# A deformable attention whose two images' and three rows' transfers are merged into single loads and stores

## The chip, the cores and the metric

The kernel runs on one core of one Trainium2 chip. The metric is device time in microseconds (us) of one execution, and the times of a kernel are given as the median of several. A core has the engines PE (TensorE, with PEld for its weight loads), DVE (VectorE), ACT (ScalarE), POOL (GpSimd) and SP (SyncE), and 16 DMA engines, which carry all transfers, whether SP, ACT or POOL issued them.

## The reference

The program is a small network over x of shape (2, 64, 64, 256): a deformable attention, a graph-routed mixture of 4 experts over 1,048,576 edges, a windowed attention, and a mixture of 8 experts. The change touches the first of the four alone:

```python
qkv = x @ qkv_w + qkv_b
qkv = _dwconv_nhwc(qkv, dw_w, dw_b)                     # depthwise 3x3, B, H, W, C = 2, 64, 64, 256
mask = einsum(pconv(q, mask_pconv_w), mask_w) + mask_b  # 9 per pixel
for g in range(8):                                      # groups of 32 channels, 9 taps each
    off = einsum(pconv(q, off_pconv_w[g]), off_w[g]) + off_b[g] + base[g]   # base: 3x3 taps, spread 2g+1
    k_g = flow_warp(k_map[group g], off) * mask         # bilinear samples of the map at the taps
    v_g = flow_warp(v_map[group g], off) * mask
attn = softmax((q / sqrt(32)) . k, over the 9 taps)
out = (attn . v) @ proj_w + proj_b
```

## The kernel before

`layernorm` (L235 to L242) and the matrix product of qkv go row by row to DRAM (`static_maps`, from L262). A second part of `static_maps` reads them back padded, makes the depthwise convolutions, and writes the maps of the attention to DRAM: queries `qd` by channel, column, row and image (L368), keys `kd` by channel and image with 16 repeated columns on each side (L434 and L436), values `vd` by group, image and row (L387), and the 153 offset and mask numbers of each pixel `offd` (L453). ACT writes each into its tile in transposed order (L366, L429, L452). In the same stretch DVE and PE sort the edges of the later mixture.

`static_attention` (from L456) then computes the attention without gathers. As an offset moves a tap by less than one pixel, the bilinear sample of a key, multiplied by the query, is a weighted sum of dot products at 3 x 3 shifts around the tap. So for each group three lanes of steps run one after another:

- `group_dots` (from L529): `queries` loads a half of the columns into `qt` (two column quarters and two images in four 32-partition blocks, one DMA each, L544), and DVE zeroes the image that a block isn't (L547). `keys` loads `kt` in the same blocks (L554, four DMAs). PE multiplies column by column (L564), ACT, at the very start also DVE, copies the result to a stage tile (L571), and ACT issues its store to `dots` in DRAM (L580).
- `group_weights` (from L590): `offsets` loads the offsets (12 DMAs, L632), `pick` and `read` load the dot products of three rows for each of the three tap rows into `lk` (L660), DVE multiplies them with the tent functions and adds (L694 to L708), takes the softmax, and forms the weights of each pixel on its 25 or 81 neighbours; POOL writes them to a matrix `wd` in DRAM (L773) and clears old ones (L788).
- `group_values` (from L842): `value_map` loads the values through `raw` (L859), DVE copies the images apart into `vt` (L861), POOL loads the matrices of `wd` into two `mat` tiles (L868), PE multiplies (L890), ACT copies the sum to `o` (L899), which has the same slot as `raw`, and issues its store to `od` (L903).

The loop `for n in range(-2, G)` takes the groups in the order 1 to 7, then 0, and runs the values of one group, the weights of the next and the dot products of the one after it in the same stage. Their steps are sorted by a fraction given by hand, and that is the order of the instructions on each engine. SP issues the loads of all three lanes in this order, so a load that waits for its buffer holds back all behind it. There are three `kt` buffers, two `qt`, two `lk`, one for offsets and one for `raw` and `o`.

`pick` has a rule for its pieces. A piece ends where the shifted row leaves the image, and one of more than 16 rows is cut to a multiple of 16:

```python
end = min(H, H - dy) if inside else (-dy if dy < 0 and y < -dy else H)
m = end - y
if m > 16:
    m -= m % 16
```

After the last group `project_out` loads `od` (L931) and multiplies by `proj_w`. A second path, `gathered` and `sample_attention`, runs only if an offset is larger than one pixel, which no input here has.

Of the kernel before, what the change touches and what calls it, by code (L numbers as in the profile page):

```python
# [23 lines left out]
F32 = mybir.dt.float32  # L24
# [97 lines left out]

def _shape_constants():
# [9 lines left out]
    grid = np.concatenate([grid.reshape(P, NOFF), np.zeros((P, K), np.float32)], 1)  # L133
# [31 lines left out]
    fold = np.concatenate([fold, own], 1)  # L165
# [15 lines left out]
class Net:  # L181
# [80 lines left out]
    def static_maps(self, maps, sort):  # L262
# [10 lines left out]
        with ExitStack() as ctx:  # L273
# [73 lines left out]
            with tc.tile_pool(name="mpad", bufs=2) as pads, tc.tile_pool(name="mq", bufs=1) as qp, \  # L347
# [12 lines left out]
                for b in range(B):  # L360
                    for j in range(CC):
                        for y in range(0, H, YC):
                            cv = kp.tile([P, YC, W], F32, name="cv")
                            self.dwconv(cv, padded("pad", j, b, y, YC), j, 0, YC)
                            to = q1[:, :, y : y + YC, b] if j else q0[:, 1 : W + 1, 1 + y : 1 + y + YC, b]
                            nc.scalar.copy(to.rearrange("p x y -> p y x"), cv)  # L366
# [43 lines left out]
                for j in range(CC):  # L410
# [5 lines left out]
                    for b in range(B):  # L416
                        km = kp.tile([P, W, H], F32, name="km", bufs=1)
                        for y in range(0, H, 8):
# [3 lines left out]
                            for tap in range(9):  # L422
# [7 lines left out]
                                km[:, :, y : y + 8].rearrange("p x y -> p y x"), ps, AF.Identity,  # L430
                                bias=bias,
                            )
                        to = kd[j * P : (j + 1) * P, b]
                        nc.sync.dma_start(to[:, BORDER : BORDER + W, :], km)  # L434
                        for at, src in ((0, 0), (BORDER + W, W - 1)):
                            nc.sync.dma_start(  # L436
                                to[:, at : at + BORDER, :], km[:, src : src + 1, :].to_broadcast([P, BORDER, H])
                            )
                XO = 8
                for x8 in range(0, W, XO):  # L440
                    off = op.tile([P, NOM, XO], F32, name="off")
                    for x in range(x8, x8 + XO, 2):
# [9 lines left out]
                        nc.scalar.copy(off[:, :, x - x8 : x - x8 + 2].rearrange("p n x -> p x n"), ps)  # L452
# [3 lines left out]
    def static_attention(self, maps, od, far):  # L456
# [7 lines left out]
        with ExitStack() as ctx:  # L464
# [12 lines left out]
            edge = one.tile([P, len(FOLDS) + B], F32, name="edge")  # L477
# [9 lines left out]
            def masks():  # L487

                masks = offd[:, NOFF:, :].rearrange("(y b) (kx ky) x -> b y ky kx x", b=B, kx=3)
                for b in range(B):  # L490
                    for ky in range(3):
                        nc.sync.dma_start(mask[H * b : H * b + H, 3 * ky : 3 * ky + 3, :], masks[b, :, ky])
                v = mask.rearrange("p (ky kx) x -> p ky kx x", ky=3)
                ob = self.row("offb")[:, NOFF:].rearrange("p (kx ky) -> p ky kx", kx=3)
                nc.vector.tensor_tensor(v, v, ob.unsqueeze(3).to_broadcast([P, 3, 3, W]), ALU.add)
                for t in mats + [none, pools["vt"]]:
                    nc.gpsimd.memset(t, 0.0)

            for n in range(-2, G):
                lanes = []  # L500
                if n >= 0:
                    g = ORDER[n]
                    lanes.append((lambda f: 0.12 + 0.88 * f, self.group_values(g, vd, wd[n % 2], mats, none, sums, od, pools)))
# [7 lines left out]
                if n + 2 < G:  # L511
                    g = ORDER[n + 2]
                    lanes.append((lambda f: 0.95 * f, self.group_dots(g, qd, kd, edge[:, len(FOLDS) :], dots, pools, n < 0)))
# [12 lines left out]
    def group_dots(self, g, qd, kd, own, dots, pools, alone):  # L526
# [12 lines left out]
        def queries(h):  # L539
            box["q", h] = qt = pools["one"].tile([P, XQ, H, B], F32, name="qt", bufs=2)  # L540
            for j in range(2):
                for b in range(B):
                    x, p0 = XH * h + XQ * j, 64 * j + 32 * b
                    nc.sync.dma_start(qt[p0 : p0 + HC], qd[g * HC : (g + 1) * HC, x : x + XQ])  # L544
# [4 lines left out]
        def keys(h, dx):  # L549
            box[h, dx] = kt = two.tile([P, XQ + 2, H], F32, name="kt", bufs=3)  # L550
            for j in range(2):
                for b in range(B):
                    x, p0 = BORDER + XH * h + XQ * j + dx, 64 * j + 32 * b
                    nc.sync.dma_start(kt[p0 : p0 + HC], kd[g * HC : (g + 1) * HC, b, x : x + XQ + 2])  # L554
# [45 lines left out]
    def group_weights(self, g, offd, mask, low, edge, s, wd, none, pools):  # L600
# [24 lines left out]
        def offsets():  # L625
            src = offd[:, g * 2 * K : (g + 1) * 2 * K, :].rearrange(
                "(y b) (kx ky two) x -> b y two ky kx x", b=B, kx=3, ky=3
            )
            for b in range(B):
                for i in range(2):  # L630
                    for ky in range(3):
                        nc.sync.dma_start(t5[H * b : H * b + H, 1, i, 3 * ky : 3 * ky + 3, :], src[b, :, i, ky])  # L632

        def bias(i):
            v = t5[:, 1, i].rearrange("p (ky kx) x -> p ky kx x", ky=3)
            ob = self.row("offb")[:, g * 2 * K : (g + 1) * 2 * K].rearrange("p (kx ky two) -> p two ky kx", kx=3, ky=3)
            nc.vector.tensor_tensor(v, v, ob[:, i].unsqueeze(3).to_broadcast([P, 3, 3, W]), ALU.add)
# [7 lines left out]
        def pick(to, dy, first, blocks, n):  # L645

            for b in range(B):
                y = 0
                while y < H:
                    ky = min(max(y + dy, 0), H - 1)  # L650
                    inside = 0 <= y + dy < H
                    end = min(H, H - dy) if inside else (-dy if dy < 0 and y < -dy else H)
                    m = end - y
                    if m > 16:
                        m -= m % 16
                    src = bass.AP(
                        s.tensor, s.offset + y * stride + b * (stride // B) + first * block + ky * line,
                        [[stride + (line if inside else 0), m], [block, blocks], [1, n * XH]],
                    )
                    nc.sync.dma_start(to[H * b + y : H * b + y + m], src)  # L660
                    y += m

        def read(ky):
            box[ky] = lk = two.tile([P, 3, 6, 3, XH], F32, name="lk")
            for sy in range(3):
                pick(lk[:, sy].rearrange("p k s x -> p k (s x)"), (ky - 1) * r + sy - 1, 0, 6, 3)

        def read_near():
            flat = two.tile([P, 27 * W], F32, name="ln", tag="lk")
            box["all"] = lk = flat[:, 0 : 25 * W].rearrange("p (y h s x) -> p y h s x", y=5, h=2, s=5)  # L670
            box["l"] = two.tile([P, 3, 6, 3, XH], F32, name="l4", tag="lk")
# [7 lines left out]
        def in_x(ky):  # L679
            tx = t5[:, :, 0, 3 * ky : 3 * ky + 3, :]  # L680
            if near:
                lk, box[ky] = box["all"], box["l"]
                for sy in range(3):
                    out = box[ky][:, sy].rearrange("p (k h) s x -> p h k s x", h=2)
# [8 lines left out]
            for sy in range(3):  # L693
                nc.vector.tensor_tensor(box[ky][:, sy], box[ky][:, sy], tx, ALU.mult)  # L694

        def sum_x(ky, i):
            l = box[ky].rearrange("p y k s x -> p (y k) s x")
            nc.vector.tensor_tensor(l[:, :, 0], l[:, :, 0], l[:, :, i], ALU.add)

        def in_y(ky):  # L700
            l = box[ky][:, :, :, 0, :]
            ty = t5[:, :, 1, 3 * ky : 3 * ky + 3, :].rearrange("p s k (h x) -> p s (k h) x", h=2)
            nc.vector.tensor_tensor(l, l, ty, ALU.mult)

        def sum_y(ky):
            l = box[ky][:, :, :, 0, :]
            nc.vector.tensor_tensor(l[:, 0], l[:, 0], l[:, 1], ALU.add)
            nc.vector.tensor_tensor(halves(lg[:, 3 * ky : 3 * ky + 3, :]), l[:, 0], l[:, 2], ALU.add)  # L708
# [90 lines left out]
        step(lambda: bias(0))  # L799
        step(lambda: bias(1))  # L800
# [41 lines left out]
    def group_values(self, g, vd, wd, mats, none, sums, od, pools):  # L842
# [11 lines left out]
        def value_map():  # L854
            wb, x0 = W + 2 * (r + 1), BORDER - (r + 1)
            for x in range(0, wb, 32):
                n = min(32, wb - x)
                raw = pools["one"].tile([P, 32, HC], F32, name="raw", tag="raw")
                nc.sync.dma_start(raw[:, 0:n, :], vd[g].rearrange("b y x c -> (b y) x c")[:, x0 + x : x0 + x + n, :])  # L859
                for b in range(B):  # L860
                    nc.vector.tensor_copy(vt[H * b : H * b + H, x : x + n, b, :], raw[H * b : H * b + H, 0:n, :])  # L861

        def load(n):
            h, kx, _ = runs[n]
            for b in range(B):
                for y in range(0, H, BAND):
                    lo, hi = band(g, y)
                    nc.gpsimd.dma_start(mats[n % 2][H * b + y : H * b + y + BAND, lo:hi], wd[y : y + BAND, b, 2 * kx + h, lo:hi])  # L868
# [28 lines left out]
        def end(h):  # L897
            o = pools["one"].tile([P, XQ, H], F32, name="o", tag="raw")
            nc.scalar.copy(o, sums[h])  # L899
            for q in range(2):  # L900
                for b in range(B):
                    x, p0 = XH * h + XQ * q, 64 * q + 32 * b
                    nc.scalar.dma_start(od[g * HC : (g + 1) * HC, b, x : x + XQ], o[p0 : p0 + HC])  # L903
# [1586 lines left out]
```

## Time and profile before

| | us |
|---|---|
| median of 3 runs | 6144.45 (6142.08 to 6149.82) |
| profiled execution, its time | 6110.76 |
| profiled execution, its span | 6109.0 |
| first attention, from the first keys load to the copy of the last group's result | 1172 to 2872 |

| engine | busy us (share of the span) |
|---|---|
| PE | 4115.2 (67%) |
| DVE | 2467.9 (40%) |
| ACT | 1154.1 (19%) |
| POOL | 1470.7 (24%) |

The profile is of one execution. A busy share is the time in which an engine had an instruction in work. A row of the groups table names a line, an engine, an operation, output <- input, their count, the busy time and mean duration, and the idle time before them with what ended it. A waits line names who waited for whom, the total, the number of waits and the longest. The DMA engines' packets are recorded with their queue (q1: SP, q10: ACT, q0: POOL), size and duration. The sum of a change is made against the profiled execution's own span; the median of the runs is 35 us above it.

### The profile page before, as it was taken

The page shows a single profiled execution, that of the slowest core. Times are in us where ns is not written, and L with a number is a line of the kernel's source. Part 1 is how long each engine was busy: PE and PEld are TensorE (multiplying, and loading weights), DVE is VectorE, ACT ScalarE, POOL GpSimd, SP SyncE. Part 2 cuts the span into 40 slices and gives each one's busy share as a digit, 9 for nine tenths or more (in the row PEclk, how much of TensorE's full clock was granted, in tenths as well). Part 3 has the DMA queues.
Part 4 walks back from the last instruction along what each step waited for, and adds up shares of the span by engine and source line. Part 5 has one row for each costly group of instructions (what it writes and reads, how often), then busy time and mean ns, then how long its engine had stood idle before and what let it go on. Part 6 is the DMA issues. An engine that isn't in the chain of part 4 may idle for free. (4 is left out here: it accounts for less than half of the span.)

```text
span 6109.0 us, 63383 instructions
## 1 busy us (share of the span) xinstructions
PE 4115.2 (67%) x22123; PEld 2876.5 (47%) x22123; DVE 2467.9 (40%) x5464; ACT 1154.1 (19%) x2302; POOL 1470.7 (24%) x1792
## 2 busy tenths in 40 slices
PE   7877688758265566354625680499947877769982
PEld 4655245745243444233412340388824444458872
DVE  6788985043121202220423473011155555532223
ACT  2110121122122222000100000122213343322210
POOL 1000001123342232443155414300062111110025
PEclk8776799868577777677867795699967888879986
DMA  6333367968678897787320001577621000058875
GB/s 179 97 102 113 99 171 148 66 152 179 126 159 175 176 188 155 120 142 126 84 13 4 4 2 64 173 225 223 194 86 40 22 21 22 21 184 263 263 235 159
DMA packets 775144, 759.72 MB, mean 124 GB/s; under 512 B 443959, under 2 KB 658935, under 8 KB 759317
## 3 DMA queue, kind: packets, MB, share of 16 engines
q1 hardware_dynamic: 576992, 412.37, 26.8%
q0 software_dynamic: 87008, 200.21, 16.9%
q10 hardware_dynamic: 110804, 142.87, 8.1%
q8 instruction: 182, 2.98, 0.2%
q14 instruction: 158, 1.29, 0.1%
HBM read 461.72 MB, written 296.60 MB: 124 GB/s over the span
## 5 line engine op out<-in xcount | busy, mean ns | idle before, releaser
L564 PE MATMUL dot<-kt,qt 64*128 64x192 f32 x2944 | 408.4, 411 | 479.1 <-ACT stage L571 320.8
L890 PE MATMUL acc<-mat,vt 128*64 128x192 f32 (+2 forms) x3680 | 491.7, 439 | 255.9 <-DMA mat<-wd 182.0
L564 PEld LDWEIGHTS dot<-kt,qt 64*128 64x128 f32 x2944 | 355.5, 235 | 535.7 <-ACT stage L571 340.5
L1658 PE MATMUL ps_h<-xgT,w1t 128*128 128x256 f32 x2240 | 545.0, 391 | 41.8 <-DVE xgT L1653 17.6
L1391 PE MATMUL ps<-oh,ol 128*128 128x512 f32 (+1 forms) x864 | 363.2, 584 | 240.8 <-issue 150.5
L1666 PE MATMUL ps_y<-w2t,hT 128*128 128x256 f32 x2240 | 513.9, 383 | 7.5 <-issue 4.4
L890 PEld LDWEIGHTS acc<-mat,vt 128*64 128x64 f32 x3680 | 310.3, 163 | 441.1 <-issue 318.1
L1658 PEld LDWEIGHTS ps_h<-xgT,w1t 128*128 128x128 f32 x2240 | 417.6, 193 | 122.8 <-DVE xgT L1653 26.2
L1666 PEld LDWEIGHTS ps_y<-w2t,hT 128*128 128x128 f32 x2240 | 430.0, 192 | 69.1 <-issue 5.2
L1661 ACT ACTIVATE hT<-ps_h,b1t 128x256 f32<-128x256 f32 x560 | 258.6, 473 | 846.4 <-PE ps_h L1658 756.7
L571 ACT COPY stage<-dot 128x384 f32<-128x384 f32 x640 | 269.5, 495 | 745.6 <-PE dot L564 295.2
L1669 DVE TENSOR_TENSOR y<-ps_y,b2t 128x256 f32<-128x256 f32 x280 | 118.8, 424 | 648.2 <-PE ps_y L1666 493.7
L1391 PEld LDWEIGHTS ps<-oh,ol 128*128 128x128 f32 x864 | 179.6, 212 | 424.0 <-issue 319.9
L868 POOL DMA_DIRECT2D mat<-wd x368 | 179.8, 494 | 590.5 <-PE acc L890 390.5
L424 PE MATMUL ps_k<-padk,diag 128*128 128x512 f32 x576 | 266.1, 621 | 76.4 <-issue 50.2
L260 DVE SCALAR_TENSOR_TENSOR cv<-pad,colt,cv 128x2048 f32<-128x2048 f32 x128 | 293.8, 2347 | 1.3
L2286 POOL DMA_INDIRECT xs<-tn,sloti x128 | 124.2, 971 | 638.9 <-DVE slot L2284 592.7
L1753 POOL DMA_INDIRECT back<-ys,back_row x128 | 123.3, 964 | 621.9 <-DVE run L2271 548.6
L1275 PE MATMUL psc<-oh,ol 128*128 128x64 bf16 x1792 | 235.0, 305 | 55.6 <-DVE oh L1273 55.6
L1275 PEld LDWEIGHTS <-ol 128*128 128x128 bf16 x1792 | 224.9, 148 | 94.0 <-issue 54.9
L333 PE MATMUL ps_q<-xT,wq 128*128 128x512 f32 x384 | 217.7, 708 | 44.5 <-ACT stage L337 33.2
L1651 PE MATMUL ps_x<-ident,xg 128*128 128x128 f32 x560 | 85.0, 275 | 225.4 <-DMA xg<-xs 225.4
(401 smaller groups left out, 6112.7 us busy)
## 6 DMA issues: line engine op xcount, KB each, us to landing
w1t<-in_W SPq DMA_DIRECT2D x140, 512.0 KB
w2t<-in_W SPq DMA_DIRECT2D x140, 512.0 KB
xg<-xs SPq DMA_DIRECT2D x140, 256.0 KB
ys<-y ACTq DMA_DIRECT2D x140, 256.0 KB
kt<-kd SPq DMA_DIRECT2D x184, 144.0 KB
pr<-stage SPq DMA_DIRECT2D x16, 1584.0 KB
mat<-wd POOLq DMA_DIRECT2D x112, 192.0 KB
mat<-wd POOLq DMA_DIRECT2D x64, 288.0 KB
```

The costliest lines, as they stand in the source:

```text
L260: nc.vector.scalar_tensor_tensor(out, src, w, out, ALU.mult, ALU.add)
L333: nc.tensor.matmul(ps.rearrange("p a b -> p (a b)"), lhsT=wq[:, k, c * P : (c + 1) * P], rhs=xT[:, k, :], start=(k == 0), stop=(k == CC - 1),)
L424: nc.tensor.matmul(ps.rearrange("p a b -> p (a b)"), lhsT=diag[:, tap, :], rhs=pad[:, at : at + 8, tap % 3 : tap % 3 + W], start=(tap == 0 ...
L564: nc.tensor.matmul(ps[jj][:, i, :], lhsT=qt[at, i0 + i].rearrange("p y b -> p (y b)"), rhs=kt[at, i0 + i : i0 + i + 3, :].rearrange("p s y ...
L571: (nc.vector.tensor_copy if alone and jj else nc.scalar.copy)(box["d"][:, :, :, x : x + 2], ps[jj].rearrange("p i (s y) -> p y s i", s=3),)
L868: nc.gpsimd.dma_start(mats[n % 2][H * b + y : H * b + y + BAND, lo:hi], wd[y : y + BAND, b, 2 * kx + h, lo:hi])
L890: nc.tensor.matmul(sums[h][64 * q : 64 * q + 64, j - 2 + a : j - 2 + c, :].rearrange("p x y -> p (x y)"), lhsT=vt[:, r + 1 + XH * h + XQ * ...
L1275: nc.tensor.matmul(psc, lhsT=ol[:, :, j], rhs=oh[:, :, j], start=(c1 == 0), stop=(c1 == NW - 1),)
L1391: nc.tensor.matmul(psf[:, c : c + m], lhsT=ol, rhs=ohf[:, c : c + m], start=(start and j == 0), stop=(stop and j == n - 1),)
L1658: nc.tensor.matmul(ps, lhsT=w1t[:, k, f * P : (f + 1) * P], rhs=xT[:, k, :], start=(k == 0), stop=(k == CC - 1),)
L1661: nc.scalar.activation(hT[:, f, :], ps, AF.Gelu, bias=b1t[:, f : f + 1])
L1666: nc.tensor.matmul(ps, lhsT=hT[:, f, i * P : (i + 1) * P], rhs=w2t[:, f, :], start=(f == 0), stop=(f == NF - 1),)
```

## The change

Storage orders change so that transfers can be joined:

- *Keys*: `kd` becomes `[G, B, HC, WB, H]`, so that a group's two images follow each other, and one DMA loads all 128 partitions of `kt`. The stores of `kd` become one for each of four groups.
- *Queries*: one DMA for each column quarter, whose source repeats the 32 channels for both images with a step of 0.
- *Picks*: `lk` is ordered `[6, 3, 3, XH]`, and one piece takes three neighbouring rows at once (9 x 32 numbers instead of 3 x 32) where none of them leaves the image; rows at the border are loaded singly. The cut to multiples of 16 rows is dropped.
- *Offsets, mask*: the rows of the offset weights and biases are sorted on the host (`_offset_order`), so that a group's 18 numbers are in the order of the tile and one DMA for each image loads them.
- *Values, matrices*: partitions are in the order (row, image) instead of (image, row). One DMA loads a band of both images of a matrix, and `value_map` separates the images by multiplying all 128 partitions with a column of ones and zeros (`odd`), so `vt` need not be zeroed once.
- *Results*: `od` becomes `[G, B, HC, W, H]`, and one DMA stores a half.
- The ACT copies of `static_maps` write in the order of the tile and read transposed.

The core of the diff:

```diff
@@ static_maps
-                            nc.scalar.copy(to.rearrange("p x y -> p y x"), cv)
+                            nc.scalar.copy(to, cv.rearrange("p y x -> p x y"))
...
-                        to = kd[j * P : (j + 1) * P, b]
-                        nc.sync.dma_start(to[:, BORDER : BORDER + W, :], km)
...
+                        for g in range(4):
+                            to, part = kd[4 * j + g, b], km[g * HC : (g + 1) * HC]
+                            nc.sync.dma_start(to[:, BORDER : BORDER + W, :], part)
...
@@ group_dots
         def queries(h):
...
             for j in range(2):
-                for b in range(B):
-                    x, p0 = XH * h + XQ * j, 64 * j + 32 * b
-                    nc.sync.dma_start(qt[p0 : p0 + HC], qd[g * HC : (g + 1) * HC, x : x + XQ])
+                src = qd[g * HC :, XH * h + XQ * j :]
+                nc.sync.dma_start(
+                    qt[64 * j : 64 * j + 64].rearrange("p x y b -> p (x y b)"),
+                    bass.AP(src.tensor, src.offset, [[0, B], [W * H * B, HC], [1, XQ * H * B]]),
+                )
...
         def keys(h, dx):
             box[h, dx] = kt = two.tile([P, XQ + 2, H], F32, name="kt", bufs=3)
-            for j in range(2):
-                for b in range(B):
-                    x, p0 = BORDER + XH * h + XQ * j + dx, 64 * j + 32 * b
-                    nc.sync.dma_start(kt[p0 : p0 + HC], kd[g * HC : (g + 1) * HC, b, x : x + XQ + 2])
+            src = kd[g, :, :, BORDER + XH * h + dx :]
+            nc.sync.dma_start(
+                kt.rearrange("p x y -> p (x y)"),
+                bass.AP(src.tensor, src.offset, [[XQ * H, 2], [WB * H, B * HC], [1, (XQ + 2) * H]]),
+            )
@@ group_weights
+            src = offd[:, g * 2 * K : (g + 1) * 2 * K, :].rearrange("(y b) n x -> b y (n x)", b=B)
             for b in range(B):
-                for i in range(2):
-                    for ky in range(3):
-                        nc.sync.dma_start(t5[H * b : H * b + H, 1, i, 3 * ky : 3 * ky + 3, :], src[b, :, i, ky])
+                nc.sync.dma_start(t5[H * b : H * b + H, 1].rearrange("p i k x -> p (i k x)"), src[b])
...
-        def pick(to, dy, first, blocks, n):
+        def pick(to, dy, first, blocks, n, y0=0, y1=H):
             for b in range(B):
-                y = 0
-                while y < H:
+                y = y0
+                while y < y1:
                     ky = min(max(y + dy, 0), H - 1)
-                    inside = 0 <= y + dy < H
-                    end = min(H, H - dy) if inside else (-dy if dy < 0 and y < -dy else H)
-                    m = end - y
-                    if m > 16:
-                        m -= m % 16
+                    inside = 0 < y + dy < H - 1
+                    end = min(y1, H - 1 - dy) if inside else (min(y1, 1 - dy) if y + dy <= 0 else y1)
                     src = bass.AP(
                         s.tensor, s.offset + y * stride + b * (stride // B) + first * block + ky * line,
-                        [[stride + (line if inside else 0), m], [block, blocks], [1, n * XH]],
+                        [[stride + (line if inside else 0), end - y], [block, blocks], [1, n * XH]],
                     )
-                    nc.sync.dma_start(to[H * b + y : H * b + y + m], src)
-                    y += m
+                    nc.sync.dma_start(to[H * b + y : H * b + end], src)
+                    y = end
 
         def read(ky):
-            box[ky] = lk = two.tile([P, 3, 6, 3, XH], F32, name="lk")
+            box[ky] = lk = two.tile([P, 6, 3, 3, XH], F32, name="lk")
+            dy = (ky - 1) * r
+            y0, y1 = max(0, 1 - dy), min(H, H - 1 - dy)
+            pick(lk.rearrange("p k y s x -> p k (y s x)"), dy - 1, 0, 6, 9, y0, y1)
             for sy in range(3):
-                pick(lk[:, sy].rearrange("p k s x -> p k (s x)"), (ky - 1) * r + sy - 1, 0, 6, 3)
+                for lo, hi in ((0, y0), (y1, H)):
+                    pick(lk[:, :, sy].rearrange("p k s x -> p k (s x)"), dy + sy - 1, 0, 6, 3, lo, hi)
@@ group_values
                 for b in range(B):
-                    nc.vector.tensor_copy(vt[H * b : H * b + H, x : x + n, b, :], raw[H * b : H * b + H, 0:n, :])
+                    nc.vector.tensor_scalar(vt[:, x : x + n, b, :], raw[:, 0:n, :], odd[:, b : b + 1], None, ALU.mult)
...
-            for b in range(B):
-                for y in range(0, H, BAND):
-                    lo, hi = band(g, y)
-                    nc.gpsimd.dma_start(mats[n % 2][H * b + y : H * b + y + BAND, lo:hi], wd[y : y + BAND, b, 2 * kx + h, lo:hi])
+            for y in range(0, H, BAND):
+                lo, hi = band(g, y)
+                nc.gpsimd.dma_start(
+                    mats[n % 2][B * y : B * (y + BAND), lo:hi].rearrange("p h s x -> p (h s x)"),
+                    wd[y : y + BAND, :, 2 * kx + h, lo:hi].rearrange("y b h s x -> (y b) (h s x)"),
+                )
...
-            for q in range(2):
-                for b in range(B):
-                    x, p0 = XH * h + XQ * q, 64 * q + 32 * b
-                    nc.scalar.dma_start(od[g * HC : (g + 1) * HC, b, x : x + XQ], o[p0 : p0 + HC])
+            to = od[g, :, :, XH * h :]
+            nc.scalar.dma_start(
+                bass.AP(to.tensor, to.offset, [[XQ * H, 2], [W * H, B * HC], [1, XQ * H]]), o.rearrange("p x y -> p (x y)")
+            )
```

## Prediction

> **What bounds the kernel now.** I first read the windows view, cut at the ends of the eight groups' results in the first attention (the copies of L899), to see which stretch the change can touch and whether an engine is full in it.
>
> ```profile
> 0.00:1172.00 1172.00, 934.75 (x4467) 642.67 (x4468) 825.08 (x1548) 200.90 (x275) 92.97 (x142) 0.82 0.54 121
> 1320.00:1532.00 212.00, 142.41 (x1022) 101.65 (x1024) 69.30 (x91) 50.16 (x114) 84.90 (x110) 0.76 0.79 157
> 1532.00:1845.00 313.00, 147.07 (x1059) 108.36 (x1055) 67.66 (x83) 64.81 (x148) 115.65 (x143) 0.70 0.73 141
> 2486.00:2663.00 177.00, 68.09 (x488) 46.66 (x486) 63.30 (x94) 5.37 (x6) 75.08 (x120) 0.69 0.83 133
> 2663.00:2787.00 124.00, 69.36 (x489) 45.51 (x489) 19.21 (x17) 2.15 (x3) 63.97 (x109) 0.75 0.73 112
> ```
>
> The columns are the window, its length, then busy us of PE, PEld, DVE, ACT and POOL, the clock, the DMA engines' mean busy share and GB/s. The stage from 1172 to 2872 us (1,700 us) holds almost all that the change edits. No compute engine is full in it: PE is busy for 142 of 212 us, 147 of 313, 68 of 177. The 16 DMA engines are busy for 0.73 to 0.83 of the time at only 112 to 157 GB/s. So this stage is bound by loads and stores and by who waits for them. The waits views of DVE, SP, ACT and PE for the same stage say which:
>
> ```profile
> DVE qt L547 <- DMA qt<-qd: 266.2, 10, 77.0
> DVE lk L694 <- DMA lk<-dots: 191.2, 30, 31.5
> DVE vt L861 <- DMA raw<-vd: 180.8, 22, 21.5
> SPq L554 <- PE dot L564: 190.0, 22, 39.0
> SPq L859 <- DMA od<-o: 150.2, 9, 96.7
> SPq L660 <- DMA lk<-dots: 91.8, 44, 8.4
> SPq L632 <- DVE wy L733: 80.8, 3, 70.3
> ACT stage L571 <- DMA lk<-dots: 159.0, 10, 28.4
> PE acc L890 <- DMA mat<-wd: 182.0, 10, 57.8
> ```
>
> Each line is total us, times, longest. DVE stands for queries, picks and values. ACT, which empties the PSUM of the dot products, stands for a *pick* of another group[...]. The DMA view of the stage gives the sizes:
>
> ```profile
> q1 hardware_dynamic: 111697, 79.74, 23.3%
> kt<-kd SPq DMA_DIRECT2D x184, 144.0 KB
> mat<-wd POOLq DMA_DIRECT2D x112, 192.0 KB
> qt<-qd SPq DMA_DIRECT2D x64, 256.0 KB
> lk<-dots SPq DMA_DIRECT2D x112, 108.0 KB
> od<-o ACTq DMA_DIRECT2D x64, 128.0 KB
> ```
>
> [...]a transfer is spread over k engines[...]. *Which* k engines are used no view shows[...]. [...]POOL's 12,288-byte matrix packets (16 partitions) have a median of 1,359 ns, ACT's packets of that size from 32 partitions 506 ns.
>
> **The change part by part.** Prices of one packet on one engine are the quickest tenth in the packet records of the stage: 4,608 B 178 ns, 8,192 B 309 ns, 4,096 B 159 ns, 384 B 22 ns, 256 B 18 ns; 1,152 B does not occur and lies between 1,024 B (46) and 1,536 B (65), so 51 ns. They are close to 26 GB/s an engine for the large ones.
>
> *Keys* (184 to 46 loads): [...]k goes from 16 to 2. One load is 128 packets of 4,608 B, 64 on each of two engines: 64 x 178 ns = 11.4 us, where the four loads before had 8 packets on each engine, 1.4 us. In all 46 x 11.4 = 524 us on engines 0 and 1.
> *Queries* (64 to 32): [...]k = 2: 32 packets x 309 ns = 9.9 us, and the two halves follow each other on the same engines, 19.8 us a query; 32 x 9.9 = 316 us.
> *Results* (64 to 16 stores on ACT): k = 2: 64 x 159 ns = 10.2 us; 163 us in all.
> *Picks of three rows* (346 + 52 near ones to 266 + 44): packets of 1,152 B instead of three of 384 B, which is cheaper per byte (51 ns against 66), but the cut to multiples of 16 rows is gone. The middle pick has 61 rows in one piece, [...]k = 1: 366 packets x 51 ns = 18.7 us, and the other image's pick follows on the same engine, 37 us. Others have 59, 53 and 47 rows (k = 1), 57 or 51 (3), 60 (15), 48 (16). Summing packets over k: 8,296 of 1,152 B, 616 of 384 B, and for the near group 880 of 384 B and 880 of 256 B fall on engine 0: 423 + 14 + 19 + 16 = 472 us. 168 of the transfers are single rows.
> *Everything else on engine 0*: stage stores and matrices 142 MB / 16 at 26 GB/s = 343 us; 33 MB of weights and cleared lines in 384-B packets, 118 us; values and offsets 40 us; together 501.
>
> Engine 0 thus has 524 + 316 + 163 + 472 + 501 = 1,976 us of work where an engine had about 700 before (the same sum with k = 16), in a stage that took 1,700. About 100 of it (two groups' matrices 45, four stores 41, last weights) falls after 2,663 us. The other 1,876 must fit where 1,491 were (1172 to 2663): at least +385. SP's two waits that no load causes, L859 for the od store and L632 for wy, 150 + 81 = 231 us, leave engine 0 without SP work, because SP issues in order and everything behind waits too. I add them: +616. Of the merged loads that share engine 0, all wait for it: matrices and stage stores with k = 16 need its sixteenth.
>
> *Matrices* (368 to 184 on POOL, 32 partitions each): 184 x 494 ns = 91 us less issuing on POOL, which idles anyway[...]. I count nothing, as engine 0 carries a share of each. Bounds: -91 and 0.
> *Offsets and mask* (102 loads to 18, k stays 16): 84 issues of about 0.6 us off SP, 50 us, and from 256-B packets to 4,608-B or 2,304-B ones. This lies within SP's waiting: 0, at best -25.
> *Values*: 48 half-width copies (632 ns mean) become 48 full-width multiplications; the row of L803, 871 ns for 1,152 elements, gives 0.8 us for 1,024: +0.15 us x 48 = +7, beside the raw loads. The od store in front of `raw`, same slot, now lands 9 us later at each group's end; inside the 616 but for the last two groups and the final store: +20.
> *Copies of static_maps* (L366 8 x 3,928 ns, L429 32 x 1,154, L452 32 x 718): the strided side changes from write to read; the trace has no such copy alone. From unchanged to halved is 0 to -46 us of ACT, of which PE's waits on them allow at most 40 (km 22 + 11, off 8); behind busy PE (935 of 1,172 us) I take -10. *Key stores* 12 to 48: k stays 16, 36 issues of 0.44 us = 16 us on an SP that has gaps there: 0 to +16, taken 0. *Bias, one memset of 5 us, loads of oT*: 0.
>
> Sum: 616 + 20 - 10 = +626 on the profiled execution's 6,109 us span, 6,735. The median of the runs shown is 35 us over that span, so 6,770; I say **6,760**.
>
> **The rivals.**
> *Spread latency*: k is small, but the engines used change from load to load. No engine fills (the mean stays near 670 us); only the latencies grow: 16 queries x 7.4 us (118), the three picks of seven groups by some 15, 8 and 3 us (182), 16 od stores x 9 (144), 444 in all, half of it behind other work: +222, 6,370. For it: no view shows engine numbers.[...]
> *Deeper convoy*: packets cost their median (256 ns at 4,608 B, 552 at 8,192 B) because queues of ACT and POOL share the two engines[...]. The moved 1,475 us (keys to picks) grow by 1.4 or more, 590 us on top of 626: 7,360. Against: the medians come from three queues being interleaved, which the sum counts already.
> *Latency hidden, matrices faster* (other side): all loads are issued early enough (three kt, two qt and lk buffers) that 11 to 37 us do not show, and the merged matrix loads halve PE's 182 us of waits: 6,144 - 91 = 6,053. It decides if a group's loads fit in its stage on the busiest engine, under about 220 us; 1,876 / 8 = 235 says no, if only just on average, and DVE waits for qt even now.
>
> **How the numbers follow.** Engine 0 bound 0.76, spread latency 0.11, convoy 0.07, hidden 0.06. The likeliest one's own range is 6,500 (the floor of +385) to 7,060 (prices a fifth higher on the moved part). The range takes in most of the spread case and stops short of the convoy: 6,350 to 7,100. About 0.2% (12 us) is what a measurement can tell from no change: faster 0.05, same 0.02, slower 0.93.
>
> **What would show it.** After: the stage from the first query to the last result takes about 2,300 us instead of 1,700; the DMA busy share falls to about 0.5 and GB/s to about 110, while SP and ACT wait for kt, qt and lk loads; q1 has few 4-byte packets; lines before 1172 us and after the first attention are unchanged. Wrong if the DVE waits on qt and lk stay near 266 and 191 us, or if the stage shrinks.

## The result and the profile after

The changed kernel takes 7,098.0 us (median of 4 runs, 7,089.5 to 7,115.1), the kernel before 6,143.3 us (4 runs on the same chip): a ratio of 1.156, 95% interval 1.153 to 1.158. The forecast was 6,760 us in a range of 6,350 to 7,100. The direction and the place were right; the size was 338 us too small. The range held the time by 2 us, above the 6,500 to 7,060 us that the prediction gave for this cause by itself, so that it lies inside is luck.

The windows view of the changed kernel, cut at its first load of `kt` and after its last result (columns as before):

```profile
0.00:1248.00 1248.00, 939.37 (x4469) 648.33 (x4470) 825.71 (x1548) 178.66 (x275) 93.43 (x142) 0.81 0.53 114
1248.00:3840.00 2592.00, 950.23 (x6687) 698.20 (x6685) 413.28 (x537) 307.90 (x681) 478.32 (x642) 0.66 0.42 100
3840.00:7087.00 3247.00, 2247.45 (x10969) 1554.92 (x10969) 1231.12 (x3371) 645.33 (x1346) 807.26 (x823) 0.82 0.37 110
```

The same view of the kernel before has for the stage:

```profile
1172.00:2872.00 1700.00, 932.26 (x6688) 677.80 (x6686) 412.39 (x545) 308.51 (x681) 573.13 (x827) 0.74 0.79 153
```

The stage of the attention grew from 1,700 us to 2,592, about 890 us. The part ahead of it grew by 76 us, and the part behind it by some 10. In the stage PE has the same work (950 us, 932 before), while the DMA engines' mean busy share is 0.42 at 100 GB/s instead of 0.79 at 153: more time, fewer busy engines. The DMA view of the stage shows q1 carrying the same bytes in half the packets, at less than half the share (10.4% against 23.3%):

```profile
q1 hardware_dynamic: 56938, 79.71, 10.4%
kt<-kd SPq DMA_DIRECT2D x46, 576.0 KB
qt<-qd SPq DMA_DIRECT2D x32, 512.0 KB
```

The waits view of the stage (total us, times, longest) for DVE, ACT, PE and SP:

```profile
DVE qt L555 <- DMA qt<-qd: 1184.2, 16, 289.0
DVE lk L700 <- DMA lk<-dots: 678.4, 41, 59.1
ACT stage L580 <- DMA lk<-dots: 622.9, 13, 77.1
PE dot L573 <- ACT stage L580: 995.0, 46, 63.8
SPq L560 <- PE dot L573: 266.3, 20, 49.1
SPq L864 <- DMA od<-o: 230.5, 6, 100.3
SPq L637 <- DVE wy L739: 194.8, 6, 62.3
```

DVE waits for queries 1,184 us instead of 266 and for picks 678 instead of 191. (289 us of the 1,184 are one wait, which begins long before the stage and ends with its first queries; in the kernel before the wait there is 176 us and stands under the name of a `kt` load, so 895 us compare with 266.) ACT waits 623 us instead of 159 for picks that it doesn't use, and PE waits 995 us for ACT. (In the trace of before the 2,480 transfers of SP and ACT name the same eight completion semaphores, 309 to 311 each. That ACT stands for a pick because it shares one with it is the author's reading.) The last three lines are SP's own waits for buffers, which matter below.

The packet records of the stage tell more than the waits. For the changed kernel:

```
q1, 1248 to 3841 us          count   quickest tenth   median
4 B                          2,810
4,608 B (keys, offsets)      6,912   178 ns           178 ns
8,192 B (queries)            2,048   312 ns           314 ns
1,152 B (picks)             14,280    51 ns            52 ns

q1 packets of 4,608 and 8,192 B in flight at once, 1248 to 3600 us:
none 1,203 us, one 307 us, two 796 us, three or more 47 us
```

They give k, the number of engines that share one transfer, as far as packets in flight together show it; that merged loads would have k = 2 was the author's estimate. In the kernel before the packets of 4,608 and 8,192 bytes are in flight for 370 us between 1172 and 2663 us, three or more of them for 287, 16 for 49 and more for 9. After the change they are hardly ever more than two, though keys of two taps and two halves of a query are often issued together. If each load took other engines and they ran side by side, four or more would be. Picks differ with the number of their rows. At 1547 us two of 61 rows, with some single rows 744 packets, take 39 us, with one packet in flight for 34 of them; at 1593 us two of 60 rows, 720 packets, take 4.3 us, with 11 or more in flight for 3; at 1793 us two of 57 rows, 686 packets, take 28 us and have three or more in flight for 11.

The 4-byte packets fit this. ACT's queue has 3,920 of them in the stage of before, 16 for each of 184 stores of dot products and 61 of results; after the change it has 2,974, which leaves 2 for each of 15 merged stores of results. On q1 the kernel before has 10,536 for SP's 772 transfers. The k of the prediction add up to 2,794 for SP's transfers after the change, and the last store of `offd` adds 16: 2,810, exactly the number found. So k is as forecast.

SP's queue taking one load after the other would look the same, so two more records of packets are needed. In queries16 (below) the queries are loaded as before the change and the keys still with k = 2. There three or more packets of queries were in flight for 102 us of the stage, and for 69 us of these one or two packets of keys ran beside them: loads of one queue do overlap. And in the changed kernel stores of results, which come from ACT's queue with k = 2, were in flight for 224 us; together with the large packets of SP's queue they were more than two for under 7 us. So large transfers with k = 2 go through the same two engines, from either queue. The records have no engine's number: "engines 0 and 1" are the author's names for these two, and "engine 0" is the busier. The picks are less clear: a packet of a pick was in flight for 511 us of 1248 to 3600, one alone for 382 of them, and a large packet beside it for only 23, though one packet in flight seems to leave the second engine free. Why was not tested.

### The profile page after: what moved, and what is told of

It is laid out like the page before. It is cut to its first block, busy times and chain, and to the rows that moved or that the text cites. A ratio compares the mean times of both kernels' runs of the same rounds, so it can differ in the third digit from the quotient of the medians.

```text
span 7087.7 us, 62659 instructions
## 1 busy us (share of the span) xinstructions
PE 4137.0 (58%) x22123; PEld 2901.4 (41%) x22123; DVE 2470.1 (35%) x5456; ACT 1131.9 (16%) x2302; POOL 1379.0 (19%) x1607
## 3 DMA queue, kind: packets, MB, share of 16 engines
q10 hardware_dynamic: 109812, 142.87, 7.4%
## 5 line engine op out<-in xcount | busy, mean ns | idle before, releaser
L573 PE MATMUL dot<-kt,qt 64*128 64x192 f32 x2944 | 428.0, 430 | 1343.7 <-ACT stage L580 995.0
L573 PEld LDWEIGHTS dot<-kt,qt 64*128 64x128 f32 x2944 | 378.4, 252 | 1397.5 <-ACT stage L580 1019.5
L555 DVE TENSOR_TENSOR qt<-qt,edge 128x2048 f32<-128x2048 f32 x16 | 36.7, 2292 | 1184.2 <-DMA qt<-qd 1184.2
L700 DVE TENSOR_TENSOR lk<-lk,tents 128x576 f32<-128x576 f32 x63 | 46.4, 757 | 705.1 <-DMA lk<-dots 678.4
L875 POOL DMA_DIRECT2D mat<-wd x184 | 90.5, 498 | 943.9 <-PE acc L900 824.1
L746 POOL TENSOR_TENSOR wt<-tents,wy 128x192 f32<-128x192 f32 x216 | 127.1, 621 | 732.9 <-DVE wy L739 705.3
```

The costliest lines, as they stand in the source:

```text
L573: nc.tensor.matmul(ps[jj][:, i, :], lhsT=qt[at, i0 + i].rearrange("p y b -> p (y b)"), rhs=kt[at, i0 + i : i0 + i + 3, :].rearrange("p s y ...
L746: nc.gpsimd.tensor_tensor(wt[ky][:, sy, :, 2 - sx, :], halves(t5[:, sx, 0, 3 * ky : 3 * ky + 3, :]), halves(box["wy"][:, sy]), ALU.mult,)
```

## The experiments

After the result three theories stood. A: the two engines that all transfers of small k share are full, and each part costs about its own work on them. B: DVE's wait of 1,184 us for queries is the queries' own, so they cost most. C: the loss comes from the other merges or from a new order of instructions. For the reading, "stage" is the time from the first load of `kt` to the copy of the last result (the views of these two tiles): 1,697 us before and 2,591 after. Single profiles of kernels whose stage should be alike differ by up to 30 us. Two sets of runs (results16, b_kd, b_copies and best; free_raw2) fell on two other chips, on which the part behind the attention takes some 280 us less (2,958 us in b_kd against 3,239 in the profile of before; the kernel before takes 5,851 and 5,841 us there), so stages, and ratios within a set, are compared, not the times of different sets.

### The four parts that lower k, mended singly and together

```diff
 keys16
+            for j in range(2):
+                src = kd[g, :, :, BORDER + XH * h + XQ * j + dx :]
+                nc.sync.dma_start(
+                    kt[64 * j : 64 * j + 64].rearrange("p x y -> p (x y)"),
+                    bass.AP(src.tensor, src.offset, [[WB * H, B * HC], [1, (XQ + 2) * H]]),
+                )
 queries16
+                for b in range(B):
+                    x, p0 = XH * h + XQ * j, 64 * j + 32 * b
+                    nc.sync.dma_start(qt[p0 : p0 + HC], qd[g * HC : (g + 1) * HC, x : x + XQ])
 picks16
+                    if end - y > 16:
+                        end -= (end - y) % 16
 results16
+            for q in range(2):
+                to = od[g, :, :, XH * h + XQ * q :]
+                nc.scalar.dma_start(
+                    bass.AP(to.tensor, to.offset, [[W * H, B * HC], [1, XQ * H]]),
+                    o[64 * q : 64 * q + 64].rearrange("p x y -> p (x y)"),
+                )
```

> The changed kernel with one edit: the load of kt is two DMAs again, one for each column quarter (64 partitions from one contiguous run of 64 rows)[...]; 92 loads instead of 46. Theory A (the two engines that the k = 2 and k = 1 loads share are full): 524 us of work fall to 65 on each of them, and most of that, some 400 us, comes off the stage: 6,650 to 6,750 us. Theory B (DVE waits for the queries, whose latency is in front of everything): keys matter little, about 7,050. Theory C (it is the new order of instructions or the other merges): about 7,100.

> The changed kernel with one edit: the load of qt is four DMAs again for each half, one for each block of 32 partitions[...]. Theory A: 316 us of work fall to 40 on the two engines, so some 270 us come off: 6,780 to 6,880 us. Theory B (DVE's wait of 1,184 us for qt is the queries' own): 500 us or more come off, 6,600 or less. Theory C: about 7,100.

> The changed kernel with one edit: a pick of more than 16 rows is cut to a multiple of 16 again (61 rows become 48 and 13), still three image rows at a time. Theory A: of the 472 us of picks on the lowest engine some 100 to 150 remain, so some 300 us come off: 6,720 to 6,850 us. Theory B: about 7,000. Theory C: about 7,100.

> The changed kernel with one edit: the result is stored by two DMAs of 64 partitions[...]. Theory A (two full engines): 163 us of work fall to 20 on the two engines, and SP's wait of 230 us for the od store in front of the next raw load gets shorter: 60 to 150 us come off, 6,950 to 7,040. Theory B' (the stores lie behind other work): less than 20 us, about 7,080. The three single edits measured so far and this one should together give about what all four gave (1,010 us).

> The changed kernel with the four edits together: keys in two DMAs, queries in four, picks cut to multiples of 16, and results in two stores of 64 partitions[...]. All other merges (offsets, mask, values, matrices, storage orders, copies) stay as in the changed kernel. Theory A: the whole loss of the stage, about 890 us, is undone, and what remains against the kernel before are the 76 us ahead of the attention and a gain of up to 90 from the matrices: 6,130 to 6,230 us. Theory B: the same. Theory C: 6,900 to 7,100.

Measured, with an estimate of the work that each edit takes off the busiest engine: the prediction's sum, packets divided by k, times the measured price of one. The k of the mended parts is the author's estimate, 16 for keys, queries and results. In all16, which has the four edits together, q10 has 110,292 packets in the whole execution and 109,812 in the changed kernel: 480 more, which is 16 for each of 32 stores of results less 2 for each of 16.

| kernel | time, us | ratio to before (95%) | stage, us | less than 2,591 by | work taken off |
|---|---|---|---|---|---|
| keys16 | 6,715.5 | 1.0957 (1.0927 to 1.0987) | 2,216 | 375 | 458 |
| queries16 | 6,795.5 | 1.1096 (1.1067 to 1.1125) | 2,285 | 306 | 276 |
| picks16 | 6,749.6 | 1.1025 (1.0993 to 1.1058) | 2,237 | 354 | 403 |
| results16 | 6,690.0 (faster chip) | 1.1457 (1.1432 to 1.1482) | 2,473 | 118 | 142 |
| all16 | 6,088.2 | 0.9935 (0.9916 to 0.9955) | 1,590 | 1,001 | 1,279 |

Each edit gives back 0.8 to 1.1 of the work that it takes off, and the edits stand in the order of their work. (The 6,950 to 7,040 us expected of results16 were meant for the other chip; the 60 to 150 us are the measure.) The four together give back all of the loss, 1,001 us where the single gains add up to 1,153. That is theory A; with all four the stage is back in the state of before, where no engine is full (about 700 us of work in 1,590, by the prediction's sum), so the last part of the sum is not paid out. B and C fall: queries alone brought 306 us, not 500, none of the edits is without effect, and all16, which keeps every other merge, has none of the stage's loss. (It came out below the 6,130 to 6,230 us expected of it; a later section shows why.)

The waits view of queries16 shows why B was tempting. Its DVE lines in the stage:

```profile
DVE lk L698 <- DMA lk<-dots: 1008.3, 44, 107.5
DVE qt L553 <- DMA qt<-qd: 419.8, 12, 277.6
```

and those of keys16, where the queries are still the slow ones:

```profile
DVE lk L701 <- DMA lk<-dots: 947.4, 42, 118.6
DVE qt L555 <- DMA qt<-qd: 394.1, 15, 112.9
DVE qt L555 <- DMA kt<-kd: 291.1, 1, 291.1
```

The wait that begins before the stage is in each of them: the 277.6 us of queries16, and the third line of keys16, where it is put down to a `kt` load. Without it DVE waits for queries 895 us in the changed kernel, 142 in queries16 and 394 in keys16. So mending the keys alone took some 500 us off the wait for queries, and in both kernels the wait for picks grew by some 300. The names in a wait say which transfer DVE stood in front of, not which one had the engine: the queries waited behind keys. Behind one full engine the waits move from one load to another.

The windows line of all16's stage has the DMA engines back at 0.73 busy:

```profile
1256.00:2847.00 1591.00, 922.21 (x6687) 653.02 (x6685) 412.98 (x537) 305.89 (x681) 482.19 (x642) 0.76 0.73 163
```

### The 76 us ahead of the attention

In the changed kernel PE stands still around 750 to 818 us. The PE line of its waits view between 600 and 1248 us, and the windows line of PE (busy us and count, clock, DMA share, GB/s):

```profile
PE ps_off L455 <- ACT q L373: 38.2, 1, 38.2
PE ps_k L431 <- ACT km L436: 25.3, 2, 23.1
```

```profile
750.00:800.00 50.00, 7.52 (x34) 0.59 0.45 137
```

The same line of the kernel before:

```profile
750.00:800.00 50.00, 45.64 (x102) 0.93 0.45 137
```

PE now meets a matmul of the offsets, for which ACT has not yet written the queries, ahead of matmuls of the keys that could run. Two parts of the change were tried alone, on the kernel before.

```diff
 b_kd: kd stored in the order group, image, channel; its loads stay four
-                        to = kd[j * P : (j + 1) * P, b]
-                        nc.sync.dma_start(to[:, BORDER : BORDER + W, :], km)
...
+                        for g in range(4):
+                            to, part = kd[4 * j + g, b], km[g * HC : (g + 1) * HC]
+                            nc.sync.dma_start(to[:, BORDER : BORDER + W, :], part)
...
 b_copies: the three ACT copies of static_maps
-                            nc.scalar.copy(to.rearrange("p x y -> p y x"), cv)
+                            nc.scalar.copy(to, cv.rearrange("p y x -> p x y"))
...
```

> The kernel before with one part of the change: kd in the order group, image, channel, stored by 48 DMAs instead of 12; the four loads of each kt stay, with k = 16. Theory O (the finer kd stores move PE's recorded order in static_maps, so that PE stands there for 60 to 80 us more): 6,195 to 6,225 us, with PE waiting for q before ps_off as in the changed kernel. Theory D (the transposed ACT copies or the full DMA engines cause the 76 us): within 15 us of 6,140.

> The kernel before with one part of the change: the three ACT copies of static_maps write in the tile's order and read transposed. The prediction took 10 us off for it (bounds 0 and 46), so 6,130 us and unclear. Theory D: slower by 60 to 80 us, 6,200 to 6,220.

b_kd: 5,922.3 us against 5,850.9 on the same chip, ratio 1.0151 (1.0127 to 1.0175), 71 us; its first load of `kt` comes at 1248.5 us and its stage is 1,702 us, as before's. The waits view of its PE between 600 and 1250 us:

```profile
PE ps_off L448 <- ACT q L366: 38.3, 1, 38.3
PE ps_k L424 <- ACT km L429: 28.0, 2, 23.2
```

These are the changed kernel's two waits. So the new order of `kd` with its finer stores brings the loss alone. PE's two waits are for ACT, not for transfers: with 48 stores in place of 12 the recorded order of PE's instructions, which none of the edited lines names, comes out differently. After the first 180 matmuls of the keys, the traces of b_kd, all16 and the changed kernel have 36 of the offsets, those of before, b_copies and best (below) have 2.

b_copies: 5,847.1 us, ratio 0.9996 (0.9985 to 1.0007), no difference, though ACT's copies did get shorter (last section). PE doesn't wait for them where it is the busy engine.

### Where all16 gains

all16 is a little faster than before although it keeps the 76 us: its stage is 107 us shorter than before's. Two merges were tried alone on the kernel before: picks of three rows with the cut to 16 kept (`pick` to `sum_y` of the change, and the two lines of picks16), and the values and matrices in the order row, image (`load`, `value_map` and `odd` of the change):

```diff
 b_picks
-            box[ky] = lk = two.tile([P, 3, 6, 3, XH], F32, name="lk")
+            box[ky] = lk = two.tile([P, 6, 3, 3, XH], F32, name="lk")
+            pick(lk.rearrange("p k y s x -> p k (y s x)"), dy - 1, 0, 6, 9, y0, y1)
...
 b_mats
-            for b in range(B):
-                for y in range(0, H, BAND):
-                    lo, hi = band(g, y)
-                    nc.gpsimd.dma_start(mats[n % 2][H * b + y : H * b + y + BAND, lo:hi], wd[y : y + BAND, b, 2 * kx + h, lo:hi])
+            for y in range(0, H, BAND):
+                lo, hi = band(g, y)
+                nc.gpsimd.dma_start(
+                    mats[n % 2][B * y : B * (y + BAND), lo:hi].rearrange("p h s x -> p (h s x)"),
+                    wd[y : y + BAND, :, 2 * kx + h, lo:hi].rearrange("y b h s x -> (y b) (h s x)"),
+                )
...
```

> The kernel before with one part of the change: lk in the order of the change and picks of three image rows at a time, with the cut to multiples of 16 rows kept[...]. The stage with all parts mended (1,590 us from the first keys load to the last result) is 107 us shorter than before's 1,697. Theory P (fewer and larger picks give that): 60 to 110 us off the stage. Theory M (the matrices of both images in one transfer give it): less than 20 us.

> The kernel before with one part of the change: values and matrices in the order row, image, so that one transfer loads a band of both images, and value_map separates the images by a multiplication. Theory M: 60 to 110 us off the stage (the prediction's rival had 91, half of PE's 182 us of waits for mat). Theory P: less than 20 us.

b_picks: 6,141.8 us, ratio 1.0002 (0.9986 to 1.0018), no difference (stage 1,727). b_mats: 6,016.5 us against 6,140.6, ratio 0.9793 (0.9761 to 0.9824), stage 1,598, so 99 us of the 107. This merge halves POOL's issues of matrices, 368 to 184, each now of 32 partitions instead of 16. It keeps k at 16: q0 has 42,080 packets in the stage instead of 45,024, so 2,944 fewer, or 16 for each issue saved. The waits view of b_mats's PE in the stage:

```profile
PE acc L896 <- DMA mat<-wd: 123.6, 12, 32.3
```

182.0 us before. The 12,288-byte packets of the matrices have a median of 889 ns (1,349 before), and the software queue q0 takes 31.6% of the 16 engines' time in the stage instead of 39.0%. Whether the packets got quicker by the partitions or by the fewer issues was not tried apart.

### A version that keeps the merges without the loss

`best` is all16 with `kd` in the order of before, so with its 12 stores. Image and channel then stand in memory as (channel, image), so the 64 rows of a load are still one run if the partitions take that order, and the query's repetition moves inside the dimension of 32 (the mask `own` becomes `odd`). The author expected k = 16 of it; the DMA engines are 0.73 busy in its stage, as in all16's.

```diff
-                    bass.AP(src.tensor, src.offset, [[0, B], [W * H * B, HC], [1, XQ * H * B]]),
+                    bass.AP(src.tensor, src.offset, [[W * H * B, HC], [0, B], [1, XQ * H * B]]),
...
-            src = kd[g, :, :, BORDER + XH * h + dx :]
+                src = kd[g * HC :, :, BORDER + XH * h + XQ * j + dx :]
```

> The changed kernel with kd in the order of before (channel, image), stored by 12 DMAs; kt is loaded by two DMAs of 64 partitions that each run through channel and image in the order they have in memory, and qt by two whose source repeats each channel with a step of 0 inside the dimension of 32 channels (partitions are channel, image in both)[...]; picks cut to multiples of 16; results in two stores. Theories A and O: what all four edits gave (6,088) less the 76 us ahead of the attention: 5,990 to 6,040 us. If D holds: about 6,085.

5,727.6 us against 5,850.9 on the same (the faster) chip, ratio 0.9814 (0.9793 to 0.9835): faster than both kernels. The expected 5,990 to 6,040 was meant for the other chip; by ratio all16 less 76 us would be 0.981. Its first load of `kt` comes at 1168.0 us, and PE is busy for 46.47 us between 750 and 800 us. But b_mats alone, one of its merges, has 0.979: all the rest of the merging, done without loss, is worth nothing that these runs show.

### SP's wait for the slot of `raw`

The prediction added SP's own waits to the engine's work. To see whether such a wait adds, two kernels leave out the copy of the result and store other values of the same size, so that `raw` has its slot to itself. In free_raw2 the store is tied to its place behind ACT's copy.

```diff
-            o = pools["one"].tile([P, XQ, H], F32, name="o", tag="raw")
-            nc.scalar.copy(o, sums[h])
+            o = pools["one"].tile([P, H], F32, name="o")
+            copied = nc.scalar.copy(o, sums[h][:, XQ - 1])
...
+                bass.AP(vd.tensor, vd[g].offset, [[XQ * H, 2], [W * H, B * HC], [1, XQ * H]]),
...
+            self.after(stored, [copied])
```

> The changed kernel with the copy of the result to o and its slot left out: ACT copies only one column of the sum to a small tile of its own and issues a store of the same bytes and shape to od, from the values in DRAM, so the two engines carry the same 163 us for it, but raw has its slot to itself and SP no longer waits for the result of the group before. It leaves out the result of the attention: what od holds is not it, and only the stage is read. Theory I (time in which SP waits leaves the two engines without work, and adds to the sum): SP's 230 us at the raw load go, and the stage falls from 2,591 to 2,360 to 2,480. Theory F (the engines are full anyway, the wait is covered by loads issued earlier): 2,550 to 2,600.

> As free_raw, with the store of od held behind the copy of the column in ACT's order, so that it stays at its place at each half's end (in free_raw ACT issued all 16 before the stage or at its start, so their work went with the wait). It leaves out the result of the attention in the same way; only the stage is read. The work on the two engines is then the changed kernel's 1,976 us, and only SP's wait of 230 us for the result in the slot of raw is taken away. Theory I (each wait of SP without a load in front adds): 2,360 to 2,480 us. Theory F (the wait is covered, the order of the other waits makes up for it): 2,550 to 2,620.

free_raw can't be read for its question: without the tie ACT issued all 16 stores between 941 and 1447 us, so their work left the stage together with the wait, and the first load of `kt` moved to 1338 us. Its stage is 2,447 us, which would lie in theory I's range, but the 144 us less are about the stores' 163. free_raw2 has the stores in place (1823 to 3868 us) and a stage of 2,619 us. SP's waits there:

```profile
SPq L560 <- PE dot L573: 501.3, 26, 62.9
SPq L637 <- DVE wy L739: 232.8, 6, 61.2
SPq L864 <- DMA raw<-vd: 173.4, 15, 43.8
```

The 230 us for `od` are gone and nothing is gained: SP waits 235 us more for PE to release `kt` buffers, and 38 more for `wy`. Theory F holds, in one run: the stage is 28 us longer than the changed kernel's, within what single profiles differ by.

## Why the prediction was right in kind and short in size

- *k and the prices*: right, but for a small term. The k of the prediction give the 2,810 4-byte packets counted; 1,152-byte packets, a price interpolated at 51 ns, take 51 ns at the quickest and 52 at the median. The weights and cleared lines are too dear: POOL's packets other than those of the matrices carry 29 MB, most of it in packets of 4,224 bytes with a quickest tenth of 164 ns, not 33 MB in packets of 384 bytes, and the same sum then gives about 93 us for them instead of 118. (The matrices' packets have a median of 1,349 ns in the stage, not 1,359.)
- *The two engines are shared and set the stage*: right. Packets in flight, from both queues, show the sharing, and the four edits show the price, each 0.8 to 1.1 of its work. The spread-latency rival needs more than two large packets in flight, from SP's queue or from SP's and ACT's together, and falls. So does the convoy rival: packets did not cost its 256 and 552 ns; medians are 178 and 314 ns, the quick prices. "Latency hidden" was on the wrong side.
- *The step that was mis-sized*: "I add them: +616", of which 231 us were SP's waits. The full sum was 1,976 us of work in a stage forecast at about 2,316, which leaves 340 us in which engine 0 has no work. The stage took 2,591, so 615 us. The 231 were before's waits, taken over as a constant, and the waits for `kt` buffers (190 us before) were left out; the prediction counted only waits "that no load causes". In the changed kernel these three lines come to 266 + 230 + 195 = 691 us instead of 421: 270 more, about the 275 missing. As an account this works on the other kernels of the set too: work left plus the three waits gives 2,169 us for keys16 (2,216 measured), 2,210 for queries16 (2,285), 2,261 for picks16 (2,237), 2,423 for results16 (2,473), 2,667 for the changed kernel (2,591) and 2,710 for free_raw2 (2,619). But it is only an account. A constant 615 us in place of the waits comes about as near (2,133, 2,315, 2,188 and 2,449 us for the four, 2,591 for free_raw2), and free_raw2 shows that the waits are not separate costs, since one that is taken away comes back at the next buffer. SP issues everything in one order, and loads wait for PE, PE for ACT, ACT for picks. Why this ring idles for some 600 us rather than 300 was not settled.
- *What was left out*: the order of PE. Key stores were priced at 0 to 16 us for 36 more issues, taken as 0; b_kd has 71 us for them. The forecast for this part was -10 and it was +76, so the sign that the lines before 1172 us stay unchanged did not hold.
- *Copies of static_maps*, -10: 0 within the interval. *Matrices*, counted as nothing: in the changed kernel they may lie hidden behind the two engines, but b_mats shows 99 us for them in the stage, the bound of 91, an estimate, to within what single profiles differ by. *Offsets and mask*: not tried alone.
- The sum: 256 us of the stage (892 against 636), 86 us ahead of it and 11 us behind it make the difference between +626 and the +979 of the profiled spans.

## What to carry to other kernels

When transfers are merged, compare how many packets of one are in flight before and after. Here the keys and queries had up to 16; with a source that begins with a dimension of 2, also one of step 0, they had two, and the large transfers of both queues met on the same two engines. Picks of 61 rows had one in flight and took 39 us for a pair, those of 60 mostly 11 or more and 4.3 us. Mending them brought 375 us for the keys, 306 for the queries and 354 for the picks. The one merge that gained here, the matrices', kept its k of 16, took 32 partitions instead of 16 and halved POOL's issues; fewer and larger picks with the cut kept gained nothing. And a wait's name is not its cause: behind one full engine, mending one load moves the wait to another, so the work taken off the busiest engine predicted the gains here (0.8 to 1.1 of it), and the waits' totals did not.

## What the runs showed of the hardware

ACT's transposing copies out of PSUM were quicker when the read was strided and the write wasn't: 512 elements per partition took 1,154 ns before and 686 ns after, 306 elements 718 and 438 ns. The copy within SBUF of 2,048 elements hardly changed, 3,928 ns before and 3,853 after. The two busy engines worked at the same price as before: 178 ns for 4,608 bytes is the quickest tenth of before and the median after.
